# Layer norms turned by VectorE and DMA instead of TensorE, in a macaron transformer layer on one Trainium2 core

## The chip, the cores and the metric

The kernel runs on one core of a Trainium2 chip (trn2). The metric is device time in microseconds (us) of one execution, taken as the median of several runs. A core has five engines that run side by side, each in the order of its own instruction list: TensorE (PE; its weight loads are listed apart as PEld), VectorE (DVE), ScalarE (ACT), GpSimd (POOL) and the queue engine SyncE (SP), which here only issues DMAs. SPq and ACTq stand for the DMAs issued from SP and from ACT.

## The reference

One layer in fp32 on x of 8 sequences, 512 tokens and 128 features: half a feed-forward, an attention with 16 heads, and half of the same feed-forward again.

```python
x = x + 0.5 * ffn(layernorm(x))
x = x + attn(layernorm(x), Q, K, VO)
x = x + 0.5 * ffn(layernorm(x))

def ffn(x):                     # three residual blocks, six 128x128 linears
    h = x
    for blk in range(3):
        y = qlora_linear(h, 2 * blk)            # int4 weights with scales + low-rank part + bias
        y = gelu(layernorm(y) * gamma[blk] + beta[blk])
        h = qlora_linear(y, 2 * blk + 1) + h
    return h
def attn(x, Q, K, VO):          # rank 64 per head
    scores = (x Q^T) (x K^T)^T / sqrt(128);  out = sum over heads of softmax(scores) x VO
```

The six weight matrices are dequantized and joined with their low-rank parts once, at the start (`wT`).

## The kernel before

All 8 sequences stay in SBUF (`xs`), token-major: partition p holds 4 tokens. The attention sets the frame. Two heads make a pair, 8 pairs a sequence, 64 pairs in all; two pairs make a **turn**, and 32 turns (numbered s = 0 to 31, four to a sequence) follow each other. A turn has eight chunks, c0 to c3 of its first and its second pair; below they are called chunks 0 to 7 of the turn. For each chunk PE computes scores `ps` (L752) into one of two PSUM buffers, tag "scores"; DVE takes the negated row maxima `nm` (L759); ACT computes `e` = exp with the row sums `den` (L764); DVE inverts them (`rden`, L771); POOL divides one half of `e` (L776) and ACT the other (L778); DVE transposes `e` in blocks of 32x32 into `tr` (L792); and 16 DMAs per pair on SP (L848) put the blocks where they belong, as `eT`. One turn later PE multiplies them with the values into `acc` (L869).

The two feed-forwards and the attention's own layer norm run in the gaps of these turns. A feed-forward of one sequence is a `Unit`: it has an input norm, three `Block`s, and a final add. In a block PE multiplies `hT` by the first weights (`py`, L387), DVE adds the bias row (`y`, L394) and takes mean and variance (L352, L354), POOL computes `rstd` by a power of -0.5 (L360), DVE subtracts the mean and scales (`z`, four instructions of 128x128, L365), PE transposes `z` in four 128x128 transposes into PSUM (`p`, L334), ACT applies gamma, beta and Gelu (`aT`, L412), PE multiplies by the second weights (`po`, L419), and DVE adds bias and residual (`hT`, L425). The input norm of a Unit goes the same way with `z_n`, `p_n`, and a copy by ACT (L431); the attention's input norm with `z_an`, `p_an` and the copy `axT` (L620). Gelu and exp need different tables on ACT: each Gelu group is followed by `exp_again`, which loads exp's table back (L187).

The order on each engine is written out by hand. `at(t, fn)` files a task under a due time t; a turn is `SUP` = 32 such units; `run_tasks` emits all tasks sorted by t, and a dependency of each instruction on the one before it on its engine keeps that order. So a due time is a place in each engine's list, not a clock: an instruction that waits holds up everything behind it on its engine. `TIMES` has the due times of the eight chunks, `T_FIRST` those of the first half of a block, and `lay_start` those of a Unit's input norm.

Which norms fall into which turn repeats every four turns. In the middle of the kernel the turns with s mod 4 = 0, 1 and 2 each turn two norms, and those with s mod 4 = 3 three: one block's, the attention's (`z_an`), and the input norm of the front feed-forward (`z_n`, due at t + 16.58, sequences 3 to 7). In turns 0 and 2 (mod 4) both are blocks' norms, scaled at the turn's start (due 35.5 to 36.2 of the turn before) and transposed together after the last scores; turn 1 has a block's and the input norm of the back feed-forward (`z_n`, due t + 4.7).

Of the kernel before, what the change touches and what calls it, by code (L numbers as in the profile page):

```python
# [18 lines left out]
def kernel(  # L19
# [45 lines left out]
    small = ctx.enter_context(tc.tile_pool(name="small", bufs=8))  # L65

# [52 lines left out]
    la = [const.tile([LR, G, D], F32, name=f"la{i}") for i in range(2)]  # L119
# [93 lines left out]
    w = [const.tile([P, G, NG, GROUP], F32, name=f"w{i}") for i in range(2)]  # L213
# [3 lines left out]
    nat = const.tile([P, 2, P], F32, name="nat")  # L217

# [120 lines left out]
    class Norm:  # L339


        def __init__(self, src, name, tag):
            self.src, self.name, self.tag = src, name, tag
# [18 lines left out]
        def scale(self):  # L362
            z = work.tile([P, NC, D], F32, tag="z", name=f"z_{self.name}")
            for c in range(self.n):
                nc.vector.tensor_scalar(  # L365
                    z[:, c, :], self.src[:, c, :], self.mv[:, c, 0:1],
                    self.rstd[:, c : c + 1],
                    ALU.subtract, ALU.mult,
                )
# [4 lines left out]


    hTs = {}

    class Block:


        def __init__(self, f, k, b, tag):
            self.k, self.b, self.tag, self.name = k, b, tag, f"{f}_{k}_{b}"

        def first(self):
            self.py = bank(f"py{self.name}", self.tag)
            for c in range(NC):
                nc.tensor.matmul(  # L387
                    self.py[:, c, :], lhsT=hTs[self.b][:, c, :], rhs=wT[:, 2 * self.k, :],
# [3 lines left out]
        def biased(self):  # L392
# [4 lines left out]
            self.norm = Norm(y, self.name, self.tag)  # L397
# [10 lines left out]

        def gelu(self):
# [3 lines left out]
                self.aT, self.norm.p, AF.Gelu,  # L413
# [15 lines left out]
    def ffn_start(n, f, b):  # L429
        hTs[b] = work.tile([P, NC, P], F32, tag="hT", name=f"hT{f}_{b}", bufs=3)  # L430
        nc.scalar.copy(hTs[b], n.p)  # L431
# [138 lines left out]
    class Unit:  # L570


        def __init__(self, f, b):
            self.f, self.b, self.tag = f, b, f"g{f}"
            self.n = Norm(xs[b], f"n{f}_{b}", self.tag)

        def lay_start(self, times, tag=None):
# [3 lines left out]
            for at_n, (fn, *args) in zip(times, (  # L581
                (self.n.stats,), (self.n.root,), (self.n.scale,), (self.n.turn,),
# [4 lines left out]
        def lay_blocks(self, s, i, other={}):  # L587
# [6 lines left out]
            for k in range(NB):  # L594
                m = Block(self.f, k, self.b, self.tag)
# [5 lines left out]
                for x, fn in zip(other.get(("second", k)) or (  # L601
                    17.65 + 0.1 * i, 22.0 + 0.1 * i, 26.0, 25.4 + 0.8 * i, 26.3 + 0.8 * i
                ), (m.turn, m.gelu, exp_again, m.second, m.add)):
                    if x:
                        at(s * SUP + x, fn)
# [8 lines left out]
    def lay_attn_input(b, t):  # L614

        n = Norm(xs[b], f"an{b}", "g0")

        def keep():
            xTs[b] = work.tile([P, NC, P], F32, tag="xT", name=f"axT{b}", bufs=2)
            nc.scalar.copy(xTs[b], n.p)  # L620
# [3 lines left out]
        at(t + 4.7, n.scale)  # L624
        at(t + 17.65, n.turn)
# [25 lines left out]
    T_EARLY, T_LATE = (28.9, 29.7, 32.3, 35.6), (31.4, 32.0, 33.8, 36.0)  # L651
    T_FIRST = (
        (T_EARLY, None), (T_EARLY, (24.2, 25.0, 26.8, 35.5)), (None, T_EARLY),
        ((25.5, 26.5, 28.5, 35.5), T_EARLY), (T_EARLY, T_LATE),
# [229 lines left out]
    def attn_add(b, a):  # L884
        oT = work.tile([P, NC, P], F32, tag="oT", name=f"oT{b}", bufs=2)
# [400 lines left out]
```

## Time and profile before

| what | value |
|---|---|
| time, median of 3 runs | 1071.25 us (1071.16 to 1071.37) |
| profiled execution, first to last instruction | 1068.9 us |
| what lies around the span, taken as median less span | 2.35 us |
| PE busy | 1053.8 us (99%), granted clock 1.000 |
| DVE busy | 873.2 us (82%) |
| ACT busy | 793.9 us (74%) |
| POOL busy | 485.1 us (45%) |
| SP's DMA queue q1 | 139.94 MB, 57.0% of 16 engines |

The profiled execution has no time of its own beside its span; the difference of 2.35 us to the median of the runs is what is assumed to lie around it. Busy time is the union of an engine's instructions. A group's line gives source line, engine, operation, output from input, shapes and count, then busy time and mean length of one; instructions of a group overlap, so four transposes take less than four times their mean length. A line of a timeline gives start, length, engine, line, operation, count, and in brackets the idle time just before it with what ended it. A line of the waits gives who waited for whom: total us, times, longest.

### The profile page before, as it was taken

How to read it: one execution, taken by the hardware profiler on the slowest of the kernel's cores; microseconds unless marked ns; L12 is line 12 of the kernel's file. 1: busy time of each engine (PE TensorE's matmuls, PEld its weight loads, DVE VectorE, ACT ScalarE, POOL GpSimd, SP SyncE). 2: the span in 40 equal slices, each digit the busy share in tenths (PEclk: the TensorE clock that was granted, in tenths of full speed). 3: DMA queues.
4: the chain of work that ended last, by engine and by line, in shares of the span. 5: the costliest groups of instructions: out<-in, count | busy, mean ns of one | idle time of the engine just before them, and what ended most of it. 6: DMA issues, size and time to landing. Idle time of an engine off the chain costs nothing.

```text
span 1068.9 us, 15650 instructions
## 1 busy us (share of the span) xinstructions
PE 1053.8 (99%) x4628; PEld 560.2 (52%) x4628; DVE 873.2 (82%) x1767; ACT 793.9 (74%) x1710; POOL 485.1 (45%) x368
## 2 busy tenths in 40 slices
PE   9899999999999999999999999999999999999998
PEld 7445554545555554555545555554555554455546
DVE  6897868788888888888889888888888888777765
ACT  4877787777777787777787777787777787777742
POOL 4554434545443454444445444455444445444423
PEclk9999999999999999999999999999999999999999
DMA  6166655665576555566455566555567555566660
GB/s 189 38 141 138 158 129 132 140 141 128 120 167 158 121 117 119 129 158 158 110 130 126 122 155 155 131 124 122 117 152 167 126 125 117 131 145 158 158 158 21
DMA packets 58572, 142.40 MB, mean 133 GB/s; under 512 B 18732, under 2 KB 22904, under 8 KB 58488
## 3 DMA queue, kind: packets, MB, share of 16 engines
q1 hardware_dynamic: 56120, 139.94, 57.0%
q10 hardware_dynamic: 2368, 1.45, 0.6%
q8 instruction: 39, 0.64, 0.3%
q14 instruction: 45, 0.37, 0.1%
HBM read 5.01 MB, written 2.10 MB: 7 GB/s over the span
## 4 chain that ended last, share of the span: by engine, by line
PE 91%; DVE 3%; ACT 2%; SPq 2%; issue 1%; DMA 0%; POOL 0%; DVEq 0%; ACTq 0%; POOLq 0%
PE acc L869 37%; PE ps L752 20%; PE pqk L689 10%; PE pv L712 10%; PE po L419 4%; PE py L387 4%; PE p L334 2%; ACT e L764 2%; PE py L489 1%; SPq L848 1%; DVE tr L792 1%; DVE nm L759 1%; SPq L824 1%; PE sum L835 1%; PE p_n L334 1%; PE ph L334 1%
## 5 line engine op out<-in xcount | busy, mean ns | idle before, releaser
L776 POOL TENSOR_SCALAR e<-e,rden 128x512 f32<-128x512 f32 x257 | 399.5, 1564 | 336.1 <-DVE rden L771 336.1
L764 ACT ACTIVATE e<-ps,nm 128x512 f32<-128x512 f32 x512 | 345.0, 685 | 157.5 <-DVE nm L759 151.5
L869 PE MATMUL acc<-eT,v 64*128 64x512 f32 (+1 forms) x1756 | 457.8, 590 | 0.7 <-DMA eT<-tr 0.7
L759 DVE TENSOR_REDUCE nm<-ps 128x2 f32<-128x1024 f32 x256 | 299.6, 1206 | 47.9 <-PE ps L752 47.7
L792 DVE STREAM_TRANSPOSE tr<-e 128x1024 f32<-128x1024 f32 x252 | 307.8, 1231 | 29.9 <-POOL e L776 21.9
L869 PEld LDWEIGHTS acc<-eT,v 64*128 64x128 f32 (+1 forms) x1756 | 192.2, 187 | 216.9 <-issue 215.1
L752 PE MATMUL ps<-qk 64*128 64x512 f32 x1024 | 248.1, 598 | 2.8 <-ACT e L764 1.8
L778 ACT ACTIVATE e<-e,rden 128x512 f32<-128x512 f32 x255 | 176.0, 726 | 15.2 <-DVE rden L771 13.9
L752 PEld LDWEIGHTS ps<-qk 64*128 64x128 f32 x1024 | 94.6, 186 | 126.2 <-issue 83.3
L712 PE MATMUL pv<-vo_sb,axT 128*128 128x256 f32 x512 | 121.7, 380 | 0.3 <-ACT e L764 0.3
L712 PEld LDWEIGHTS pv<-vo_sb,axT 128*128 128x128 f32 x512 | 94.8, 190 | 28.7 <-issue 12.4
L360 POOL TENSOR_TENSOR rstd<-mv,mhalf 128x4 f32<-128x4 f32 x42 | 42.9, 1022 | 146.7 <-DVE mv L354 145.9
L764 ACT ACTIVATION_READ_ACCUMULATOR e<-ps,nm 128x1 f32 x512 | 103.6, 202 | 0.0
L725 ACT COPY v<-pv 128x512 f32<-128x512 f32 x124 | 66.8, 594 | 42.0 <-PE pv L712 42.0
L771 DVE RECIPROCAL rden<-den 128x2 f32<-128x2 f32 x256 | 41.4, 165 | 36.3 <-ACT e L764 35.4
L695 ACT COPY qk<-pqk 128x1024 f32<-128x1024 f32 x61 | 61.0, 1000 | 3.9 <-PE pqk L689 3.9
L689 PE MATMUL pqk<-axT,qT_w 128*128 128x512 f32 x122 | 63.3, 601 | 0.2 <-ACT e L764 0.2
L689 PE MATMUL pqk<-axT,kT_w 128*128 128x512 f32 x122 | 62.3, 592 | 0.0
L387 PEld LDWEIGHTS py<-wT,hT 128*128 128x128 f32 x336 | 42.3, 191 | 13.0 <-DVE hT L425 9.2
L365 DVE TENSOR_SCALAR z<-y,mv,rstd 128x128 f32<-128x128 f32 x168 | 48.1, 356 | 0.6 <-POOL rstd L360 0.6
L394 DVE TENSOR_TENSOR y<-py,bias_bc 128x512 f32<-128x512 f32 x42 | 28.7, 683 | 22.6 <-PE py L387 22.0
L387 PE MATMUL py<-wT,hT 128*128 128x128 f32 x336 | 45.4, 278 | 1.0 <-DVE hT L425 0.8
(143 smaller groups left out, 724.0 us busy)
## 6 DMA issues: line engine op xcount, KB each, us to landing
eT<-tr SPq DMA_DIRECT2D x1008, 128.0 KB, 2.3
x<-in_L_attn_x_dram SPq DMA_DIRECT2D x7, 256.0 KB, 6.0
out_dram<-x SPq DMA_DIRECT2D x7, 256.0 KB, 2.4
eT<-tr SPq DMA_DIRECT2D x16, 64.0 KB, 2.0
eT<-tr ACTq DMA_DIRECT2D x16, 64.0 KB, 2.1
qk_sb<-in_L_attn_Q_dram SPq DMA_DIRECT2D x1, 448.0 KB, 4.4
qk_sb<-in_L_attn_K_dram SPq DMA_DIRECT2D x1, 448.0 KB
x<-in_L_attn_x_dram SPq DMA_DIRECT2D x2, 128.0 KB, 2.8
```

The lines of the kernel that those rows point to most:

```text
L387: nc.tensor.matmul(self.py[:, c, :], lhsT=hTs[self.b][:, c, :], rhs=wT[:, 2 * self.k, :], start=True, stop=True,)
L689: nc.tensor.matmul(self.pg[:, i, :], lhsT=(qT_w, kT_w)[i][:, self.g, :], rhs=xTs[self.b], start=True, stop=True,)
L695: nc.scalar.copy(self.qk, self.pg)
L712: nc.tensor.matmul(p, lhsT=xTs[self.b][:, c, :], rhs=vo_sb[:, 2 * self.g : 2 * self.g + 2, :], start=True, stop=True,)
L725: nc.scalar.copy(self.v[:, c : c + NC // 2], self.pv[:, c : c + NC // 2])
L752: nc.tensor.matmul(ps[:, j, :], lhsT=self.qk[rows, 0, ts(c, P)], rhs=self.qk[rows, 1, :], start=True, stop=True,)
L759: nc.vector.tensor_reduce(self.nm[:, c, :], self.ps[c], AX.X, ALU.max, negate=True)
L764: nc.scalar.activation(e[:, j, :], self.ps[c][:, j, :], AF.Exp, bias=self.nm[:, c, j : j + 1], accum_out=self.den[:, c, j : j + 1],)
L776: nc.gpsimd.tensor_scalar(e, e, r, None, ALU.mult)
L778: nc.scalar.activation(e, e, AF.Copy, scale=r)
L792: nc.vector.transpose(self.tr[:, :, :, c, :], self.e[c].rearrange("p h (k j r) -> p j (h k) r", j=Q4, r=32),)
L869: nc.tensor.matmul(accs[self.b][i], lhsT=self.v[rows, k, j, :], rhs=self.eT[rows, :, j * NC + k, :], start=first, stop=end and (j == 1 or ...
```

## The change

Three things are changed. First, the norms that are transposed for a turn s > -1 (all but the input norms of sequences 1 and 2 of the front feed-forward, the first block of sequence 1, and the last block of sequence 6 of the back one) are no longer transposed by PE. VectorE transposes `z` in 32x32 blocks into a buffer `zout` (`spread`, one instruction of 128x512). Once per turn an `Exchange` writes the buffer of all its norms (two or three of 256 KB) to DRAM with one DMA, and reads it back with four DMAs, one for each 32 partitions, such that the blocks land transposed (`zin`). All five are issued from SP, due at 8.0 of the turn. ACT's Gelu and copies read `zin` in SBUF instead of `p` in PSUM.

Second, `z` of these norms is computed on GpSimd instead of VectorE. Input norms still subtract and scale; blocks' norms only multiply by `rstd`, since the first weights and biases are centred once at the start (`sums`, `centered`): each output column's mean over the features is taken away, so that `y` has mean zero. Due times move: the scaling follows the root at once, `spread` is due 3.6 to 3.7 into the turn (5.45 for the back feed-forward's block in turns 3 mod 4, 7.5 for its input norm). The front feed-forward's input norm has its statistics moved one turn ahead (due 26.9 of turn s-2, where it was 27.0 of turn s-1), its root and scaling to 16.0 of turn s-1.

Third, room is made: the start's weight tiles `la` and `w` share a buffer with the exchange (tag "zx"), and `oT` has one buffer instead of two.

```diff
+        dram = tc.tile_pool(name="dram", bufs=2, space=bass.MemoryType.DRAM)
+    def sums():
+        first = wT.rearrange("p (k two) o -> p k two o", two=2)[:, :, 0, :]
+        for i, src in enumerate((first, bias_bc)):
+            nc.vector.tensor_reduce(less[:, i, :], src, AX.X, ALU.add)
+    def centered():
+        nc.gpsimd.tensor_scalar(less, less, -1.0 / D, None, ALU.mult)
+        for i in range(2):
+            for k in range(NB):
+                nc.gpsimd.tensor_scalar(
+                    bias_bc[:, k, :] if i else wC[:, k, :],
+                    bias_bc[:, k, :] if i else wT[:, 2 * k, :],
+                    less[:, i, k : k + 1], None, ALU.add,
+                )
...
         def scale(self):
+            engine = nc.gpsimd if self.exchange else nc.vector
             for c in range(self.n):
-                nc.vector.tensor_scalar(
+                if self.centered:
+                    engine.tensor_scalar(
+                        z[:, c, :], self.src[:, c, :], self.rstd[:, c : c + 1], None, ALU.mult
+                    )
+                    continue
+                engine.tensor_scalar(
                     z[:, c, :], self.src[:, c, :], self.mv[:, c, 0:1],
                     self.rstd[:, c : c + 1],
                     ALU.subtract, ALU.mult,
...
+        def spread(self):
+            nc.vector.transpose(
+                self.exchange.out()[:, :, self.slot, :, :],
+                self.z.rearrange("p c (j r) -> p j c r", r=32),
+            )
+        def turned(self):
+            if self.exchange:
+                return self.exchange.landed[:, :, self.slot, :, :].rearrange("p i c q -> p c i q")
+            return self.p.rearrange("p c (i q) -> p c i q", q=32)
+    class Exchange:
...
+        def run(self):
+            f = self.n * NC * 32
+            far = dram.tile([P, Q4, f], F32, tag="far", name=f"far{self.s}")
+            nc.sync.dma_start(out=far, in_=self.sent.rearrange("p j a c q -> p j (a c q)"))
+            self.landed = self.tile("zin")
+            for j in range(Q4):
+                nc.sync.dma_start(
+                    out=self.landed[32 * j : 32 * (j + 1)].rearrange("p i a c q -> p i (a c q)"),
+                    in_=far.rearrange("(i r) j f -> j r i f", r=32)[j],
+                )
+    SPREAD = (3.6, 3.7)
...
-                    self.py[:, c, :], lhsT=hTs[self.b][:, c, :], rhs=wT[:, 2 * self.k, :],
+                    self.py[:, c, :], lhsT=hTs[self.b][:, c, :], rhs=wC[:, self.k, :],
...
-                self.aT, self.norm.p, AF.Gelu,
+                self.aT.rearrange("p c (i q) -> p c i q", q=32), self.norm.turned(), AF.Gelu,
...
+                    if far and fn == m.turn:
+                        at(s * SUP + (5.45 if i and s % 4 == 3 else SPREAD[i]), m.spread)
...
-        at(t + 4.7, n.scale)
-        at(t + 17.65, n.turn)
+        at(t + 0.3, n.scale)
+        at(t + 3.65, n.spread)
...
-    T_EARLY, T_LATE = (28.9, 29.7, 32.3, 35.6), (31.4, 32.0, 33.8, 36.0)
+    T_EARLY, T_LATE = (28.9, 29.7, 32.3, 32.4), (31.4, 32.0, 33.8, 33.9)
...
+    at(-0.55, sums)
+    at(-0.5, centered)
...
-            m.lay_start((t - 5.0, t + 1.1, t + 16.58, t + 20.3, t + 20.7))
+            m.lay_start((t - 2 * SUP + 26.9, t - SUP + 16.0, t - SUP + 16.1, t + 3.6, t + 20.7))
...
-            m.lay_start((t + 0.1, t + 1.1, t + 4.7, t + 17.65, t + 17.85))
+            m.lay_start((t + 0.1, t + 1.1, t + 1.2, t + 7.5, t + 17.85))
```

## The prediction

> **What bounds the kernel now.** I read the page first, then the groups, then the list of waits, and then the timeline of whole turns, engine by engine.
>
> The page's busy line (us, share of the span, instructions) names TensorE, and the largest group of transposes that the change removes (busy us, mean ns, idle us before) sits on it:
>
> ```profile
> PE 1053.8 (99%) x4628; PEld 560.2 (52%) x4628; DVE 873.2 (82%) x1767; ACT 793.9 (74%) x1710; POOL 485.1 (45%) x368
> ```
> ```profile
> L334 PE MATMUL p<-ident,z 128*128 128x128 f32 x168 | 24.4, 279 | 1.3 <-DVE z L365 1.3
> ```
>
> Read alone, this says that every us taken from PE is a us gained. The list of waits (total us, times, longest) says something else:
>
> ```profile
> ACT aT L412 <- PE p L334: 13.3, 1, 13.3
> ...
> PEld pqk L689 <- ACT qk L695: 11.8, 27, 0.6
> ...
> PEld po L419 <- ACT aT L412: 6.8, 22, 1.0
> ```
>
> Gelu waited for PE's transposes once in 42 times (at the start), but PE's weight loads waited for Gelu's result 22 times and for ACT's copy of q and k 27 times. The order in time shows why. Turn 8 (s mod 4 = 0, from 275.9 us), PE and its weight loads, then ACT:
>
> ```profile
> 293.36 1.09 PE L334 MATMUL p<-ident,z 128*128 128x128 f32 x8
> 294.29 3.60 PE L869 MATMUL acc<-eT,v 128*128 128x512 f32 x8
> ...
> 301.16 1.92 PE L419 MATMUL po<-aT,wT 128*128 128x512 f32 x4
> ```
> ```profile
> 301.10 0.30 PEld L419 LDWEIGHTS po<-aT,wT 128*128 128x128 f32 x2 [0.18 <-ACT aT L412]
> ...
> 302.67 0.44 PEld L689 LDWEIGHTS pqk<-axT,qT_w 128*128 128x128 f32 x2 [0.42 <-ACT qk L695]
> ```
> ```profile
> 294.78 0.69 ACT L764 ACTIVATE e<-ps,nm 128x512 f32<-128x512 f32 x1 [0.85 <-DVE nm L759]
> ...
> 298.98 1.28 ACT L412 ACT_TABLE_LOAD   x1
> ...
> 300.27 1.45 ACT L412 ACTIVATE aT<-p,gb 128x512 f32<-128x512 f32 x2
> ...
> 301.61 1.01 ACT L695 COPY qk<-pqk 128x1024 f32<-128x1024 f32 x1
> ```
>
> From 294.78 to 302.6 ACT has no gap: exps of chunks 6 and 7, two divisions, table, two Gelus, copy of q and k. PE needs the Gelus for `po` and the copy for its next scores buffer. So the second half of a turn is set by when DVE releases chunk 6 (the 0.85 us wait for `nm`), and PE, which had the transposes to do meanwhile, arrives at `po` within 0.1 us of ACT. Two chains of equal length run there, and only one gets shorter.
>
> Where does chunk 6's `nm` wait? In turns 8, 9 and 10 it follows DVE's own `tr` without a gap; in turn 11 (s mod 4 = 3) something of the change stands before it. DVE and ACT of turn 11:
>
> ```profile
> 388.05 1.23 DVE L792 STREAM_TRANSPOSE tr<-e 128x1024 f32<-128x1024 f32 x1
> 389.20 1.19 DVE L365 TENSOR_SCALAR z_n<-x,mv_n,rstd_n 128x128 f32<-128x128 f32 x4
> 390.32 2.34 DVE L759 TENSOR_REDUCE nm<-ps 128x2 f32<-128x1024 f32 x2
> ```
> ```profile
> 391.62 0.69 ACT L764 ACTIVATE e<-ps,nm 128x512 f32<-128x512 f32 x1 [1.23 <-DVE nm L759]
> ```
>
> **The change, part by part.** Everything is summed against the profiled span, 1068.9 us; the median of the runs is 2.35 us more.
>
> *PE's transposes removed.* 59 norms (40 of blocks, 7 of the attention, 5 and 7 input norms) times four are 236 transposes. Eight hold PE from 293.36 to 294.29, 0.116 us each, so 27.4 us of PE. On the path I count what PE's arrival was late: `pqk` started at 302.93 where the copy ended at 302.62 and its weights could load at 302.67, so about 0.07 us a turn, 30 turns: -2.0 us. Ends: 0 and -27.4. I take the low one because the two weight loads above already wait for ACT.
>
> *`z_n` leaves DVE before chunk 6.* The four scalings take 389.20 to 390.32, 1.12 us, straight on the chain `tr`, `nm`, exp, table, Gelu, `po`. The scores of chunk 6 are there sooner: PE began them at 387.30, the first half takes 0.86. PE follows, as without its twelve transposes it ends `acc` at about 391.6. This happens in the turns of sequences 3 to 7: 5 x 1.12 = -5.6 us. End: 0, if ACT's `axT` copy, which stands before exp 6, has to wait for its data instead.
>
> *Other scalings leave DVE, `spread` comes.* One `tr` of 128x1024 is 1.23 us, so a `spread` of 128x512 is about 0.62 (0.75 with a fixed part). In turn 10 eight scalings took 2.13 us after the first two `nm`; two spreads take 1.25. But the next `nm` waited 0.6 us for PE's scores there, so nothing comes of it: 0. In turn 9 the later `spread` of the back input norm comes between `nm` of chunk 3 and its `rden`, where DVE waits 0.44 us for exp: 0.62 less 0.44 eats the 0.2 us that chunk 2's `nm` gains. 0.
>
> *GpSimd's scaling, and who waits for it.* In turn 11 POOL's list now reads root (attention), four scalings with two operations, root (block), four with one, and only then the first division:
>
> ```profile
> 371.22 1.03 POOL L360 TENSOR_TENSOR rstd_an<-mv_an,mhalf 128x4 f32<-128x4 f32 x1 [7.05 <-DVE mv_an L354]
> 372.99 1.01 POOL L360 TENSOR_TENSOR rstd<-mv,mhalf 128x4 f32<-128x4 f32 x1 [0.74 <-DVE mv L354]
> ...
> 377.06 1.58 POOL L776 TENSOR_SCALAR e<-e,rden 128x512 f32<-128x512 f32 x1 [2.09 <-DVE rden L771]
> ```
>
> A division of 512 columns takes 1.56 us. A quarter of it is 0.39; with a fixed part of about 0.12 (two memsets, 24 columns 0.141 us and 216 columns 0.278) it is 0.48. That is my value for one operation; for two I take 0.60, between 0.48 and twice that. 371.22 + 1.03 + 2.40 + 1.01 + 1.94 = 377.6, and the block's `spread` ends at 378.2; DVE's `nm` of chunk 2 stands behind it and began at 378.35. So 0, with ends: scalings at 0.39 let it start when PE's scores are there (378.05), 7 x -0.3 = -2; at 0.53 and 0.97 the `spread` ends at 379.9, 7 x 1.5 = +10.8. In other turns POOL has at most one norm before a `spread`, and the first `tr` comes 3 us after its division, so a division 0.5 us late is hidden. The root and scaling of the front input norm, moved to 16.0 of turn 10, fall between 358.25 and 361.07, where POOL is idle 2.81 us; they need 3.4, so division 6 is 0.6 late, `tr` of chunk 7 too, and behind it `hT`, which waited 0.78 for PE: hidden. Its statistics (1.25 us) go into a gap of DVE of 1.25 us in turn 9.
>
> The Trainium skill, page "GPSIMD Engine Reference", section "Engine selection", speaks against this step: elementwise work belongs on VectorE, with GpSimd about twice as slow for two inputs and near line rate for one. Its section "Performance versus the Vector engine" measures 769 ns for 512 elements in the best case, and by that a scaling would be an estimated 0.19 us and the term -2; the division's 1.56 us in this trace is twice the page's figure, and the trace decides.
>
> *The exchange.* 59 x 256 KB go out and come back, some 30 MB beside q1's 140. SP gets five issues a turn at about 0.6 us each, and its four reads wait for the write to land. In turn 9, the tightest, the last `spread` ends at about 317.5; SP is idle from 314.5 to 325.8. A 256 KB store lands in 2.4 us, so 512 KB in about 3.6; four reads of 128 KB are issued in 2.4 and the last lands 2.3 (as `eT`) to 3.3 later: 325.2 to 326.5. SP is free again at 323.5, before the next `eT` DMA. ACT's copy of `hT`, due before exp 6, must start by 326.3. I take 0.1 us of wait in seven such turns: +0.7; ends 0 and +7 (reads 1 us later). In turn 11 768 KB land at about 388.8, needed at 389.7. In turns 8 and 10 the Gelus come at 300 and 364, with 7 us to spare.
>
> *ACT reads SBUF.* A division by ACT (SBUF, 726 ns) against an exp (PSUM, 685 ns), both with a column operand, gives 0.04 us more; 40 Gelus on ACT's chain: +1.6. Ends: 0, and 0.11 (0.61 between two divisions against 0.50 between two copies of v), +4.4.
>
> *Start.* `sums`, two reductions of 128x384, stand directly before the first `nm` (29.73, right behind `z_n`). At `nm`'s 1.2 us per 1024 columns that is 0.5 us each: +1.0 (ends +0.5, +1.5). `centered` lies in POOL's idle time up to 32.8 and delays a first division by 1 to 2 us, which its `tr` at 41.19 doesn't notice.
>
> Sum: -2.0 - 5.6 + 0 + 0 + 0.7 + 1.6 + 1.0 = -4.3: a span of 1064.6, a time of 1067.
>
> **The rivals.**
>
> *PE is the bound, as its 99% says.* Then all 27.4 us less the start's 1.0 are gained: 1045. For it: PE has 15 us of gaps in the whole span. Against: the waits of its weight loads, which the busy share hides.
>
> *GpSimd holds DVE (slower).* In the three-norm turns DVE waits at the block's `spread` with `nm`, and with it exp, queued behind. Each us that POOL's eight scalings take beyond 4.3 delays seven turns, and beyond 5.1 us (0.48 for one operation, 0.8 for two) it eats the 5.6 us. At 6.0 us: -4.3 + 10.8 = +6.5, 1078. For it: the division is slow on POOL. Against: 0.48 leaves 0.15 us to spare.
>
> *The round trip is late.* If the reads land 1.5 us later than reckoned, turns with a copy before exp 6 lose some 1.3 us: 7 x 1.3 in turns 1 mod 4, and the 5.6 of turns 3 mod 4 shrink to 2: -4.3 + 8.4 + 3.6 = +7.7, 1079. Against: DRAM traffic is only 7 GB/s, and SP is idle when it is issued.
>
> *Nothing is left.* Gelu from SBUF at its upper end, and 0.5 us lost in turn 9, cancel the gain: 1071.
>
> **How the numbers follow.** Chances: forecast 0.42, PE bound 0.08, GpSimd 0.22, round trip 0.15, nothing 0.13. This measurement tells 0.2%, about 2.1 us, from no change. Faster: the forecast and the PE case, 0.50. Same 0.14: the case of nothing left, and a little from the slower ones. Slower 0.36. The likeliest case alone reaches from 1059 to 1071. The range runs to 1049, leaving only the full PE case below, and to 1083, where GpSimd's upper end (+10.8) meets some of the others' costs.
>
> **What would show it.** Right: PE's busy share falls by some 2.5 points while `po` and `pqk` wait longer for ACT, about 0.9 us a turn; in turns 3 mod 4 exp 6 starts about 1.1 us earlier after the turn's first scores. Wrong: PE still without waits and the span down by 20; DVE's `spread` waiting for POOL's `z`; ACT's `axT` or `hT` waiting for a DMA; the start waiting on weights, whose tiles now share a buffer.

## The result, and the profile after

| | before | after |
|---|---|---|
| time, median (lowest to highest) | 1071.37 us (1071.13 to 1073.08, 9 runs) | 1073.01 us (1072.66 to 1076.57, 9 runs) |
| ratio to before | | 1.0025, 95% interval 1.0014 to 1.0035 |
| profiled execution, first to last instruction | 1068.9 us | 1071.0 us |

The changed kernel is a little slower: +1.6 us by the medians, +2.1 us between the two profiled executions, where -4.3 had been forecast. The measured direction is that of the rival "GpSimd holds DVE". The page's line on the engines, after (us, share of the span, instructions):

```profile
PE 1041.5 (97%) x4392; PEld 534.2 (50%) x4392; DVE 843.9 (79%) x1592; ACT 792.3 (74%) x1710; POOL 642.2 (60%) x611
```

PE is busy 12.3 us less and DVE 29.3 us less; POOL is busy 157 us more. In the chain of work that ended last, before and then after (shares of the span by engine):

```profile
PE 91%; DVE 3%; ACT 2%; SPq 2%; issue 1%; DMA 0%; POOL 0%; DVEq 0%; ACTq 0%; POOLq 0%
```
```profile
PE 49%; DVE 16%; ACT 12%; SPq 10%; POOL 5%; DMA 4%; issue 4%; DVEq 0%; ACTq 0%; POOLq 0%
```

PE alone carried the end before; now PE shares it with DVE, ACT and POOL. The changed kernel's list of waits says who waits for whom (total us, times, longest). PE's weight loads wait for Gelu 21.0 us in 40 places, where it was 6.8 in 22, and VectorE's `spread` (`zout`) waits for GpSimd's scalings:

```profile
PEld po L508 <- ACT aT L501: 21.0, 40, 1.5
PEld pqk L784 <- ACT qk L790: 14.0, 27, 0.6
```
```profile
DVE zout L408 <- POOL z L393: 12.4, 9, 1.5
DVE zout L408 <- POOL z_an L397: 4.0, 5, 1.3
```

**Where the time went, turn by turn.** From the start of each turn's first scores on PE to that of the next, summed by s mod 4 (turns 0 and 1 apart), profiled executions:

| us | before | after | difference |
|---|---|---|---|
| up to the first scores | 28.39 | 28.90 | +0.51 |
| turns 0 and 1 | 63.54 | 64.64 | +1.10 |
| seven turns s mod 4 = 0, from 4 | 219.63 | 218.48 | -1.15 |
| seven turns 1, from 5 | 217.06 | 215.11 | -1.95 |
| eight turns 2 | 251.37 | 250.02 | -1.35 |
| seven turns 3 | 223.58 | 228.11 | +4.53 |
| from the last turn's first scores to the end | 65.33 | 65.74 | +0.41 |

The turns 0, 1 and 2 mod 4 that transpose two norms each got 0.2 to 0.3 us shorter. Of the turns 3 mod 4, numbers 11, 15, 19 and 23 take 32.91 us instead of 32.27, and number 27, which has no `z_n`, 32.38 instead of 30.58. (Number 3 takes 32.08 instead of 31.64, and number 7, which has `z_n`, 32.03 instead of 32.27.)

**A turn with two norms** (turn 8, PE, its weight loads and ACT in the changed kernel; start, length, operation, in brackets the idle time before it and what ended it):

```profile
302.07 1.98 PE L508 MATMUL po<-aT,wT 128*128 128x512 f32 x4 [0.34 <-ACT aT L501]
```
```profile
302.07 0.30 PEld L508 LDWEIGHTS po<-aT,wT 128*128 128x128 f32 x2 [0.74 <-ACT aT L501]
302.78 0.45 PEld L508 LDWEIGHTS po<-aT,wT 128*128 128x128 f32 x2 [0.41 <-ACT aT L501]
```
```profile
295.72 0.69 ACT L859 ACTIVATE e<-ps,nm 128x512 f32<-128x512 f32 x1 [0.85 <-DVE nm L854]
...
301.20 1.52 ACT L501 ACTIVATE aT<-zin,gb 128x512 f32<-128x512 f32 x2
302.63 0.99 ACT L790 COPY qk<-pqk 128x1024 f32<-128x1024 f32 x1
```

PE, rid of its eight transposes, now waits for Gelu before `po`; ACT runs from exp 6 on without a gap, as before. The 0.85 us wait for `nm` is the same to the digit.

**A turn with three norms** (turn 11, POOL and DVE in the changed kernel):

```profile
371.62 1.03 POOL L386 TENSOR_TENSOR rstd_an<-mv_an,mhalf 128x4 f32<-128x4 f32 x1 [5.65 <-DVE mv_an L380]
373.39 1.01 POOL L386 TENSOR_TENSOR rstd<-mv,mhalf 128x4 f32<-128x4 f32 x1 [0.73 <-DVE mv L380]
374.40 3.13 POOL L397 TENSOR_SCALAR z_an<-x,mv_an,rstd_an 128x128 f32<-128x128 f32 x4
377.51 2.36 POOL L393 TENSOR_SCALAR z<-y,rstd 128x128 f32<-128x128 f32 x4
```
```profile
377.57 0.71 DVE L408 STREAM_TRANSPOSE zout<-z_an 128x512 f32<-128x512 f32 x1 [0.67 <-POOL z_an L397]
...
379.90 0.71 DVE L408 STREAM_TRANSPOSE zout<-z 128x512 f32<-128x512 f32 x1 [1.51 <-POOL z L393]
380.54 2.31 DVE L854 TENSOR_REDUCE nm<-ps 128x2 f32<-128x1024 f32 x2
```

The maxima of chunk 2 before the change:

```profile
378.35 2.33 DVE L759 TENSOR_REDUCE nm<-ps 128x2 f32<-128x1024 f32 x2
```

From 372.65 to 373.39 POOL waits for the block's `mv`, and the attention norm's scaling, whose data are there, is queued behind that wait. The two scalings then take 3.13 and 2.36 us. VectorE waits 0.67 and 1.51 us at its two `spread`s, and `nm` of chunk 2 begins 8.39 us after the turn's first scores (372.15); before it was 6.60 (378.35 less 371.75). That is 1.79 us later.

### The profile page after: what moved, and what is told of

Its sections match the earlier page's. It is cut to its first block, busy times and chain, and to the rows that moved or that the text cites. A ratio compares the mean times of both kernels' runs of the same rounds, so it can differ in the third digit from the quotient of the medians.

```text
span 1071.0 us, 15598 instructions
## 1 busy us (share of the span) xinstructions
PE 1041.5 (97%) x4392; PEld 534.2 (50%) x4392; DVE 843.9 (79%) x1592; ACT 792.3 (74%) x1710; POOL 642.2 (60%) x611
## 3 DMA queue, kind: packets, MB, share of 16 engines
q10 hardware_dynamic: 2368, 1.45, 0.6%
## 4 chain that ended last, share of the span: by engine, by line
PE 49%; DVE 16%; ACT 12%; SPq 10%; POOL 5%; DMA 4%; issue 4%; DVEq 0%; ACTq 0%; POOLq 0%
PE acc L964 17%; PE ps L847 11%; SPq L943 9%; DVE tr L887 7%; ACT e L859 7%; PE pqk L784 6%; DVE nm L854 5%; PE pv L807 5%; PE po L508 4%; DMA eT<-tr 3%; ACT L501 2%; POOL z L393 2%; PE py L473 2%; POOL z_an L397 2%; ACT aT L501 1%
## 5 line engine op out<-in xcount | busy, mean ns | idle before, releaser
L847 PE MATMUL ps<-qk 64*128 64x512 f32 x1024 | 252.2, 602 | 8.8 <-ACT e L859 7.0
L807 PEld LDWEIGHTS pv<-vo_sb,axT 128*128 128x128 f32 x512 | 94.7, 190 | 29.3 <-issue 8.9
L393 POOL TENSOR_SCALAR z<-y,rstd 128x128 f32<-128x128 f32 x160 | 94.3, 609 | 3.3
L866 DVE RECIPROCAL rden<-den 128x2 f32<-128x2 f32 x256 | 36.4, 144 | 50.4 <-ACT e L859 49.4
L508 PE MATMUL po<-aT,wT 128*128 128x512 f32 x84 | 43.9, 627 | 7.3 <-ACT aT L501 7.2
L473 PEld LDWEIGHTS py<-wC,hT 128*128 128x128 f32 x336 | 42.3, 191 | 12.3 <-DVE hT L514 7.1
L473 PE MATMUL py<-wC,hT 128*128 128x128 f32 x336 | 45.1, 277 | 0.9 <-DVE hT L514 0.9
```

The source lines that it names most:

```text
L393: engine.tensor_scalar(z[:, c, :], self.src[:, c, :], self.rstd[:, c : c + 1], None, ALU.mult)
L473: nc.tensor.matmul(self.py[:, c, :], lhsT=hTs[self.b][:, c, :], rhs=wC[:, self.k, :], start=True, stop=True,)
L807: nc.tensor.matmul(p, lhsT=xTs[self.b][:, c, :], rhs=vo_sb[:, 2 * self.g : 2 * self.g + 2, :], start=True, stop=True,)
L847: nc.tensor.matmul(ps[:, j, :], lhsT=self.qk[rows, 0, ts(c, P)], rhs=self.qk[rows, 1, :], start=True, stop=True,)
```

## The experiments

Each kernel is a change of one of the two kernels. Runs of before on the same chips had medians of 1071.17 to 1071.50 us; the ratios are against them.

### e1: the block's spread behind the scores of the second pair

```diff
-  at(s * SUP + (5.45 if i and s % 4 == 3 else SPREAD[i]), m.spread)
+  at(s * SUP + (7.5 if i and s % 4 == 3 else SPREAD[i]), m.spread)
```

> The changed kernel with one due time moved: in the turns 3 mod 4 the block's spread is due 7.5 instead of 5.45, so it stands behind the maxima of chunks 2 and 3 instead of ahead of them. Theory H (GpSimd holds DVE: the spread waits 1.5 us for POOL's z, with nm and exp queued behind): chunk 2's nm starts 2.1 us sooner, the spread itself costs 0.2 us later, and the exchange is sent some 2 us later, which may make ACT's axT copy wait 0.5 us: 1.4 us in each of seven turns, 1060 to 1064 us instead of 1073. Rival T (the round trip through DRAM is late): sending it later makes it worse, up to 7 x 1.2, 1073 to 1081. Rival P (PE is the bound): 1073.

Measured: 1062.13 us (1060.98 to 1064.06), ratio 0.9916 (0.9901 to 0.9930). The seven turns 3 mod 4 take 216.77 us instead of 228.11: -11.3 us, 1.6 us in each on average (0.9 in turn 7, 1.5 to 1.9 in the others); every other group of turns stays within 0.15 us but turn 0, of which more below. VectorE in turn 11 (first scores at 371.12):

```profile
377.45 2.36 DVE L854 TENSOR_REDUCE nm<-ps 128x2 f32<-128x1024 f32 x2
379.72 0.70 DVE L408 STREAM_TRANSPOSE zout<-z 128x512 f32<-128x512 f32 x1
```

`nm` comes 6.33 us after the first scores, ahead of the `spread`, and the `spread` follows it without a wait, with POOL's list and GpSimd's durations unchanged. One due time thus turns the change from 0.25% slower to 0.8% faster. The hold is shown, and its size: 11.3 us is what the place of this `spread` ahead of `nm` cost. What is late next shows in the waits of ACT in e1 (none of this kind in the changed kernel):

```profile
ACT axT L715 <- DMA zin<-far: 5.0, 5, 1.1
```

The later `spread` sends the exchange off later, and in the five turns with `z_n` the copy `axT` now waits about 1 us for the round trip. PE in turn 11 of e1 has no wait in its second half, so this one is hidden there.

### e6: only the order on POOL

```diff
-        at(t + 0.3, n.scale)
+        at(t + 0.25, n.scale)
```

> The changed kernel with one due time altered: the attention norm's scaling at t + 0.25 instead of t + 0.3, so that on POOL it stands ahead of the block's root, which waits for VectorE's mv. Theory (the order on POOL's list is part of the hold): z_an starts at the end of its own root (372.7 instead of 374.4 in turn 11), the block's root follows at about 375.8, its four scalings end at about 379.1 instead of 379.9, so the block's spread and nm of chunk 2 come 0.7 to 1.1 us earlier in seven turns: -5 to -7.5 us, a time of 1065.5 to 1068. Rival (the order doesn't matter, since POOL's work up to the block's spread is as much in either order, and only the scalings' size counts): the turns 3 mod 4 stay at 32.9 us, 1073.

Measured: 1070.51 us (1068.44 to 1072.56), ratio 0.9992 (0.9982 to 1.0002). POOL in turn 11 (first scores at 371.32):

```profile
371.93 3.13 POOL L397 TENSOR_SCALAR z_an<-x,mv_an,rstd_an 128x128 f32<-128x128 f32 x4
375.03 1.03 POOL L386 TENSOR_TENSOR rstd<-mv,mhalf 128x4 f32<-128x4 f32 x1
376.16 2.36 POOL L393 TENSOR_SCALAR z<-y,rstd 128x128 f32<-128x128 f32 x4
```

`z_an` starts 1.64 us earlier in the turn's own time (0.61 us after the first scores instead of 2.25), but the block's root now stands behind it and starts at 375.03 instead of at 373.39. POOL ends the block's scaling at 378.5, and `nm` begins 7.86 us after the first scores instead of 8.39. The turns 11, 15, 19, 23 and 27 get 0.52 us shorter, turn 7 1.0, the group 3.6 us in all. (The median moves by 2.5 us only, since more of its executions fell under the drop of the clock told of below.) So the order is about a third of the hold; the lower end of what was expected was 0.7 us a turn. The rest of the hold is put down to the scalings' length; no run has shorter scalings on GpSimd.

### e2: the transposes put back on PE, unread

```diff
     if far and fn == m.turn:
         at(s * SUP + (5.45 if i and s % 4 == 3 else SPREAD[i]), m.spread)
+        at(s * SUP + x, m.turn)
...
+    if self.n.exchange:
+        at(times[4] - (0.2 if self.f else 0.4), self.n.turn)
...
     at(t + 3.65, n.spread)
+    at(t + 17.65, n.turn)
```

> The changed kernel with the 236 TensorE transposes put back at their old due times, writing to PSUM banks that nobody reads; everything else as changed. Two equal chains (PE had these transposes while ACT was on its way to Gelu, so taking them away was worth 0.07 us a turn): 0 to +3 us, 1073 to 1076. Rival P (PE is the bound, and the 27 us were gained and lost again elsewhere): +27, 1100.

Measured: 1082.94 us (1082.62 to 1085.27), ratio 1.0115 (1.0099 to 1.0132): +9.9 us on the changed kernel, +9.8 between the profiled spans (1080.8 against 1071.0). The turns 0, 1 and 2 mod 4 with two norms get 0.2 to 0.3 us longer, the five with three 0.89; numbers 3 and 27, which have two, do not change. This lies between the two theories: the transposes hold PE for 27 us, a good third of it was on the path, and my 0.07 us a turn was far too little.

### e7: both, the late spread and the transposes on PE

> The kernel of e1_late_spread, in which VectorE no longer waits for GpSimd, with the 236 transposes on PE put back beside the exchange, their result unread. It shows what they are worth once the hold is gone. Theory (the chain through DVE and ACT and PE's own work are nearly equal in every turn, so each part of the change is worth something only where the other has shortened its chain too): +0.25 us in turns 0, 1 and 2 mod 4 as in e2, and +1.0 or more in turns 3 mod 4, where the chain is now 1.8 us shorter and twelve transposes are 1.4 us of PE: +13 to +16 us on 1062, that is 1075 to 1078. Rival (what the transposes cost does not depend on the hold): +9.9 us, 1072. Rival (PE alone is the bound): +27, 1089.

Measured: 1071.48 us (1070.28 to 1076.79), ratio 1.0007 (0.9994 to 1.0020). By groups of turns, against e1 and against before:

| us | before | e1 | e7 |
|---|---|---|---|
| turns 0 mod 4 | 219.63 | 218.44 | 219.60 |
| turns 1 mod 4 | 217.06 | 215.26 | 217.02 |
| turns 2 mod 4 | 251.37 | 249.97 | 251.31 |
| turns 3 mod 4 | 223.58 | 216.77 | 222.50 |

With the transposes back, three of four groups are as before within 0.06 us: the exchange, the scalings on GpSimd and the `spread`s, without PE's relief, are worth nothing there and cost nothing. The transposes are worth 10.0 us over the four groups without the hold (e7 less e1) and 9.1 with it (e2 less the changed kernel). The 0.9 us between them are mainly the net of two things. Turn 5, which varies between 29.2 and 29.9 us among the profiled executions, counts 0.7 less without the hold than with it. The turns 3 mod 4 count 1.35 more, and most of that is one turn: number 15 of e7 takes 33.03 us where 7, 11, 19 and 23 take 32.10 to 32.11. ACT's timeline has there

```profile
523.22 0.62 ACT L718 COPY axT<-zin 128x512 f32<-128x512 f32 x1 [2.82 <-DMA zin<-far]
```

which is the round trip again, this time not hidden. The `spread` is no later there than in e7's other turns; the write took longer: the four reads, which wait for it, were issued 5.07 us after it (517.51 and 512.44), against 3.30 us in turn 11 of e1. Why it took longer is open. In the four other turns with three norms the transposes cost 0.88 to 1.01 us, about as in e2. So the theory was wrong and the rival right: what PE's transposes cost hardly depends on the hold. The waits of `po` for `aT` and of `pqk` for `qk`, 21.0 and 14.0 us in the changed kernel, in e7:

```profile
PEld po L508 <- ACT aT L501: 6.1, 19, 1.1
PEld pqk L788 <- ACT qk L794: 8.3, 23, 0.6
```

They are back at or below the 6.8 and 11.8 us of the kernel before: with the transposes PE is the later one in most turns.

### e3: z_n off VectorE, the transposes kept

The kernel before, with the front norm's statistics, root and scaling moved one turn ahead and the scaling on GpSimd.

```diff
+  engine = nc.gpsimd if self.ahead else nc.vector
...
-  m.lay_start((t - 5.0, t + 1.1, t + 16.58, t + 20.3, t + 20.7))
+  m.n.ahead = True
+  m.lay_start((t - 2 * SUP + 26.9, t - SUP + 20.9, t - SUP + 20.95, t + 20.3, t + 20.7))
```

> The kernel before with one part of the change alone: the front feed-forward's input norm (sequences 3 to 7) has its statistics, root and scaling one turn earlier, the scaling on GpSimd where POOL is idle after the last division (due 20.95), so that no z_n stands before the maxima of chunk 6 on DVE. TensorE still transposes. The prediction's step: 5 x 1.12 us, 1071.4 - 5.6 = 1065.8. Rival P: PE's work is the same, 1071.4.

Measured: 1071.33 us (1070.64 to 1073.12), ratio 0.9999 (0.9990 to 1.0008). VectorE does what was expected of it: in turn 11 (first scores at 373.92) the second half's `nm` follows `tr` directly, and exp 6 starts 1.1 us earlier in the turn. The turn gets 0.16 us shorter (32.10 instead of 32.26). PE in turn 11 of e3, and then of before:

```profile
394.80 0.60 PE L334 MATMUL p_n<-ident,z_n 128*128 128x128 f32 x4
...
398.68 1.06 PE L390 MATMUL py<-wT,hT 128*128 128x128 f32 x8
399.57 1.02 PE L422 MATMUL po<-aT,wT 128*128 128x512 f32 x2
400.43 1.02 PE L692 MATMUL pqk<-axT,qT_w 128*128 128x512 f32 x2
```
```profile
392.62 0.60 PE L334 MATMUL p_n<-ident,z_n 128*128 128x128 f32 x4
...
396.67 1.05 PE L387 MATMUL py<-wT,hT 128*128 128x128 f32 x8
397.63 1.12 PE L419 MATMUL po<-aT,wT 128*128 128x512 f32 x2
398.60 1.07 PE L689 MATMUL pqk<-axT,qT_w 128*128 128x512 f32 x2
```

In neither does PE wait (no brackets): with twelve transposes to do, PE arrives at `po` when the Gelus are there anyway. Exp 6 waiting 1.23 us for `nm` was true, but PE did not wait behind it. The seven turns 3 mod 4 together get 0.8 us shorter, the four groups only 0.2.

### e4: the round trip left out

```diff
-            at(s * SUP + 8.0, x.run)
+            at(s * SUP + 8.0, x.stay)
...
+        def stay(self):
+            self.landed = self.sent
```

> The changed kernel without the exchange: no DMA out and none back, ACT reads the spread blocks as they lie in zout. This leaves out the crossing of blocks between partitions, so what is computed is not the reference. Theory H: no instruction of ACT waited for the trip in the profile, so only SP's issues and some 30 MB of DMA traffic go: 0 to -2 us, 1071 to 1073. Rival T: the trip holds ACT's copies in the turns 1 and 3 mod 4, -7 us or more, 1066 or less.

Measured: 1074.99 us (1073.36 to 1076.91), ratio 1.0033 (1.0020 to 1.0046). All groups of turns are within 0.2 us of the changed kernel's: as it was changed, the trip through DRAM costs nothing in them. The kernel is not faster but 2 us slower by the median; in the profiled execution this lies in the last 30 us: PE waits longer for the last `eT` there (2.59 us instead of 1.72) and then runs slowly, which no theory had foreseen. Its one execution without such a slow stretch took 1073.4 us, 0.4 to 0.7 us above those of the changed kernel. The last two groups of experiments are about that.

### e5 and e8: what is left on POOL, and the start

e5 is e1 with the order of e6 and the front norm's root and scaling moved behind the last division of their turn (from due 16.0 and 16.1 to 20.9 and 20.95).

> The kernel of e1_late_spread (block's spread in turns 3 mod 4 due 7.5 instead of 5.45), with POOL's list reordered in two places: the attention norm's scaling ahead of the block's root (t + 0.25 instead of t + 0.3), and the front input norm's root and scaling due 20.9 and 20.95 of the turn before instead of 16.0 and 16.1, behind the last division. Theory: the hold is gone already by the later spread, so nothing is left to gain there; the division of chunk 6 in turns 2 mod 4 is no longer 2 us late, but this was hidden; 1060 to 1063, equal to e1 within 1 us. Rival (GpSimd's divisions still delay DVE's tr): another 0.3 us in five to seven turns, 1058 to 1060.

Measured: 1064.71 us (1062.80 to 1065.47), ratio 0.9931 (0.9917 to 0.9944). The four groups of turns take 900.8 us, those of e1 900.4: nothing is left to gain on POOL, as expected. The time is 2.6 us above e1's nevertheless, and its reason lies elsewhere: in the profiled execution 2.3 us before the first scores (30.96 us instead of 28.65). All five of its executions also show a drop of the clock, of e1's four only two; see below for both.

e8 is e5 with the centring moved; `sums` and `centered` are split there into the weights' part (0) and the biases' (1):

```diff
-    at(-0.55, sums)
-    at(-0.5, centered)
+    at(1.2, sums, 0)
+    at(1.25, centered, 0)
+    at(3.85, sums, 1)
+    at(5.45, centered, 1)
```

> e5_combined with the centring at the start moved: the sums of the weights between the first two nm (due 1.2), those of the biases at 3.85, GpSimd's additions behind them (1.25 and 5.45), so that the first nm follows z_n directly, as before the change. Theory: the 0.83 us that turn 0 lost come back mostly, 0.5 to 1 us on e5_combined. Rival (py, which needs the centred weights, then waits for GpSimd, as it began at 38.13 and the additions end at about 36): nothing gained or up to 1 us lost.

Measured: 1062.13 us (1060.93 to 1063.04), ratio 0.9913 (0.9899 to 0.9926). Turn 0 takes 30.49 us; it was 31.19 in the changed kernel and 30.36 before, so 0.7 of the 0.8 us come back. `py` did not wait for the centred weights. The median moves by 2.6 us, more than was expected of the start: only two of e8's four executions show a drop of the clock.

### e9 and e10: the clock

In e1, e5 and e7 turn 0 took 32.6 us instead of the changed kernel's 31.2, with the same instructions. PE in turn 0 of the changed kernel, and then of e5:

```profile
33.91 1.13 PE L847 MATMUL ps<-qk 64*128 64x512 f32 x4 [1.44 <-ACT e L859]
35.25 1.13 PE L847 MATMUL ps<-qk 64*128 64x512 f32 x4 [0.21 <-ACT e L859]
36.31 1.12 PE L767 MATMUL pq<-axT,qT_w 128*128 128x512 f32 x2
```
```profile
35.97 1.13 PE L847 MATMUL ps<-qk 64*128 64x512 f32 x4 [1.43 <-ACT e L859]
37.31 1.71 PE L847 MATMUL ps<-qk 64*128 64x512 f32 x4 [0.21 <-ACT e L859]
38.95 2.07 PE L767 MATMUL pq<-axT,qT_w 128*128 128x512 f32 x2
```

The same matmuls after the same wait take up to 1.8 times as long. The windows of e5 (window, length, busy time of PE, PEld, DVE, ACT, POOL, then the granted clock, DMA share and GB/s) show why, and those of e6 show the same at the end of the kernel:

```profile
33.00:37.00 4.00, 2.57 (x12) 0.84 (x12) 2.73 (x4) 2.97 (x9) 3.50 (x7) 1.00 0.00 0
37.00:42.00 5.00, 4.79 (x12) 1.82 (x11) 3.81 (x8) 3.50 (x10) 4.69 (x5) 0.66 0.00 0
```
```profile
1036.00:1040.00 4.00, 1.79 (x6) 0.73 (x5) 2.94 (x14) 0.00 (x0) 1.03 (x1) 1.00 0.71 173
1040.00:1044.00 4.00, 4.00 (x14) 3.29 (x13) 0.00 (x0) 0.00 (x0) 0.00 (x0) 0.57 0.14 33
```

Us by us the clock stands at 0.50 for some 3.4 us and then at 1.00 again. Two waits of PE come before it: one of 1.44 us in turn 0, because the first `nm` stands behind the two `sums` (before the change it was 0.51), and one of 1.6 to 2.6 us for the last `eT` at the end (1.56 before the change). In the profiled executions the drop came after a wait of 1.44 us in turn 0 (e1, e5, e7) and after waits of 2.2 to 2.6 us at the end (e4, e6, e7). To test whether PE's idleness is the cause, e9 fills the second wait, and e10 both, with matmuls that nobody reads; e9 starts from e8, e10 from e5, whose late start stays.

```diff
+    for i in range(10):                                   # e9, e10
+        at(t + 19.9, lambda: nc.tensor.transpose(end_sums[1][:, :P], ident, ident))
...
+    for i in range(10):                                   # e10
+        at(1.96, lambda: nc.tensor.transpose(first.p[:, 3, :], first.z[:, 3, :], ident))
```

> The kernel of e8_start (late spread, POOL's order, centring moved) with ten transposes of the unit matrix on PE, their result unread, ahead of the ten sum matmuls at the end, where PE waits 1.7 to 2.6 us for the last eT DMAs. Theory (a wait of PE of 1.4 us or more is what lets the granted clock fall to 0.50 some us later, in part of the executions): the wait shrinks to about 0.6 us, and no execution shows a mean clock under 0.9995: its times lie at 1060.5 to 1061.5 without the ones at 1063. Rival (the clock falls for another reason, or at any wait there): the times still spread over 2 us, 1062.

> The kernel of e5_combined (centring still ahead of the first nm) with ten such transposes at the end as in e9_filled and ten more in turn 0, behind p_n, where PE waits 1.44 us for exp. Nothing at the start is sooner: the first nm still stands behind the two sums. Theory (it is PE's idleness that drops the clock, not the late start itself): turn 0 takes 31.2 us in every execution, never 32.6, the mean clock is 1.000, and the time is that of e9 plus the 0.7 us by which turn 0 is longer: 1061 to 1062.5. Rival: turn 0 still takes 32.6 us in part of the executions, 1063 to 1065 as e5.

Measured: e9 1061.62 us (1060.74 to 1064.16), ratio 0.9911 (0.9896 to 0.9926); e10 1062.01 us (1061.36 to 1064.62), ratio 0.9914 (0.9899 to 0.9928). PE at the end of e9:

```profile
1029.37 1.26 PE L1260 MATMUL sum<-ident 128*128 128x128 f32 x10
1031.02 2.40 PE L928 MATMUL sum<-eT,v 128*128 128x256 f32 x10 [0.39 <-issue]
```

The mean granted clock of each execution tells the rest:

| kernel | executions with a mean clock under 0.999 | times at 0.999 or more | times under 0.999 |
|---|---|---|---|
| before, beside e1 to e10 | 0 of 44 | 1070.6 to 1073.4 | |
| after | 4 of 9 | 1072.7 to 1073.0 | 1075.0 to 1076.6 |
| e1 | 2 of 4 | 1061.0 to 1062.0 | 1062.3 to 1064.1 |
| e2 | 2 of 4 | 1082.6 to 1082.7 | 1083.2 to 1085.3 |
| e3 | 0 of 10 | 1070.6 to 1073.1 | |
| e4 | 4 of 5 | 1073.4 | 1073.9 to 1076.9 |
| e5 | 5 of 5 | | 1062.8 to 1065.5 |
| e6 | 7 of 11 | 1068.4 to 1069.4 | 1070.4 to 1072.6 |
| e7 | 4 of 11 | 1070.3 to 1071.7 | 1073.3 to 1076.8 |
| e8 | 2 of 4 | 1060.9 to 1061.3 | 1062.9 to 1063.0 |
| e9 | 0 of 5 | 1060.7 to 1064.2 | |
| e10 | 0 of 5 | 1061.4 to 1064.6 | |

With the waits filled no mean clock was under 0.999 (one in e9 was 0.999, the others 1.000; the drop of 3.4 us alone makes 0.998), and e10's turn 0 took 31.20 us although its first `nm` is as late as e5's: it is PE's waiting that lets the clock fall. What decides between two executions with the same wait can be read off the profiled ones, though no run tests it. In their records of the granted clock every stretch between two changes is a whole multiple of 3.413 us (1064.96 us is 312 of them, 27.31 is 8), so the clock changes on a grid of that period, and the grid lies differently against the kernel in each execution. At the end e5, e6 and e7 wait 2.21 us each. In e6 and e7 2.1 us or more of it fell into one period of the grid, and the clock dropped at that period's end; in e5 the grid cut the wait in two, 1.48 us the larger part, and it did not drop. In turn 0 it dropped where one period held 1.64 us or more without a matmul (e1, e5, e7), not where it held 1.62 or less (the changed kernel, e2, e4, e6); that margin is thin, and at the end 1.96 us (e2) were not enough, so no single number follows.

The times of e9 and e10 still spread by more than 3 us, as e9's rival had it, though not for its reason: some are 2 us and more above the rest at full clock, as are some of the kernel before (1073 among 1071). In the profiled executions of e3, e5 and e7 the first scores began some 2 us later than elsewhere (30.55 to 30.96 us instead of 28.4 to 29.2). The same matmul early in the kernel before, and then in e3:

```profile
5.98 0.27 PE L478 MATMUL pp<-ident,pz 128*128 128x128 f32 x1
```
```profile
7.00 0.42 PE L481 MATMUL pp<-ident,pz 128*128 128x128 f32 x1
```

The records of the granted clock begin, at 1.00, when the matmuls get short: at 10.0 to 10.5 us in e3, e5 and e7, at 3.9 to 6.4 us in the nine others. So PE starts slow in every profiled execution and in these three stays so for 3.5 us or more longer; the mean granted clock, which counts from the first record on, does not show it (e3: 1.00). That this is also what e9's and e10's longer times are was not seen in a profile.

e8 and e9 are the best versions found, 0.9% under the kernel before and 1.0% under the changed one; e1, with one due time changed, and e10 are equal to them within the intervals.

## Why the prediction was wrong, point by point

**GpSimd's scalings (forecast 0, measured +11.3 us: the step that failed).** This term alone decides the direction: without the hold the change is 0.8% faster (e1). Two errors add up. The lengths: I took 0.48 us for a scaling with one operation and 0.60 for one with two. The group of the changed kernel's POOL (busy us, mean ns of one; overlapping instructions, so four take 2.36 and 3.13 us):

```profile
L871 POOL TENSOR_SCALAR e<-e,rden 128x512 f32<-128x512 f32 x257 | 399.4, 1567 | 218.7 <-DVE rden L866 218.5
L393 POOL TENSOR_SCALAR z<-y,rstd 128x128 f32<-128x128 f32 x160 | 94.3, 609 | 3.3
L397 POOL TENSOR_SCALAR z_an<-x,mv_an,rstd_an 128x128 f32<-128x128 f32 x28 | 21.9, 797 | 0.1
```

They are 0.59 and 0.78 us. For a quarter of the division's columns that is a fixed part of about 0.27 us ((4 x 0.59 - 1.56) / 3), twice what I had drawn from two memsets, and a second operation costs 0.19. Eight scalings took 5.49 us instead of 4.34, 1.15 more. The order: I listed root, scaling, root, scaling, but by the due times (the block's root is due 32.3 of the turn before, the attention norm's scaling 0.3 of this one, filed later) both roots come first, and the second waits for VectorE. e6 gives 0.52 us for it. Together 1.67 us; less the 0.15 us of slack that is 1.52 of the 1.79 us by which `nm` moved. The rival had the mechanism, the place and the price (+10.8 at its upper end); its lengths were given as the range's end (0.53 and 0.97), and its sum was +6.5, 4 to 5 us too much, because it took over the forecast's too small gain from PE's transposes. That its price came out is in part luck: its lengths add up to 6.0 us for the eight scalings, and the measured 5.49 us comes to that only with the wait that the order added. Both were within reach: "0.15 us to spare" on a path of 6.4 us is no cover. The Trainium skill, page "GPSIMD Engine Reference", section "Engine selection", says that elementwise work belongs on VectorE, and the trace agrees: the four scalings of `z_n` took 1.12 us there, and 3.13 on GpSimd. The best case of its section "Performance versus the Vector engine", an estimated 0.19 us for a scaling, was missed by a factor of three.

**PE's transposes (forecast -2.0, measured -9 to -10 us).** That PE would then wait for Gelu was right: 0.74 and 0.41 us at the weight loads of `po` in turn 8, and not all 27 us were gained. The mechanism was right too; the term was mis-sized: I read how late PE was in one turn (0.07 us, turn 8) and took it for all. Gelu and `po` of turn 12, before (first scores at 404.02) and after (405.06):

```profile
428.00 1.45 ACT L412 ACTIVATE aT<-p,gb 128x512 f32<-128x512 f32 x2
429.19 1.88 PE L419 MATMUL po<-aT,wT 128*128 128x512 f32 x4
```
```profile
429.04 1.52 ACT L501 ACTIVATE aT<-zin,gb 128x512 f32<-128x512 f32 x2
429.91 1.98 PE L508 MATMUL po<-aT,wT 128*128 128x512 f32 x4 [0.34 <-ACT aT L501]
```

Gelu starts 23.98 us after the first scores in both, `po` 25.18 and then 24.85 us after them, and `pqk` behind it 26.89 and then 26.67. So PE came 0.33 us late to `po` and 0.22 late to `pqk`, and the turn got 0.23 us shorter. In e7's turn 19, with twelve transposes, `po` comes 0.76 us later in the turn than in e1's, while Gelu starts within 0.03 us of it; that turn is 0.90 us longer.

**z_n off VectorE (forecast -5.6, measured -0.8 alone).** The 0.8 us are those of the turns 3 mod 4; the time did not change. The wait of exp 6 was real and went away (in e3's turn 11 exp 6 follows the copy `axT` without a wait, where it waited 1.23 us), but PE, busy without a gap from 388 to 404 us, set the end of that turn. I had followed the chain to `po` in turn 8 and assumed it in turn 11. Only with both parts, and without the hold, do the turns with three norms lose 1.0 to 1.3 us (e1). The two terms together were forecast at -7.6; the four groups of turns of e7's table add up to 911.6 us before and 900.4 in e1, -11.2. So the gain was there, and larger than forecast, but for another reason: nearly all of it comes from PE's transposes. Over the whole span the -11.2 us and the hold's +11.3 cancel, and +1.6 at the start and +0.4 at the end make the +2.1 us.

**The exchange (forecast +0.7, measured 0).** e4 shows that the turns do not depend on it. ACT never waited for `zin`; 512 KB landed 2.8 us after their issue, and the four reads 2.8 after theirs. The rival's mechanism is real, though: where the write is issued 0.8 us later in the turn and the copy is due sooner, as in e1 and e7, `axT` waits for the reads.

**The `spread`s, Gelu from SBUF, other edits at nothing.** A `spread` took 0.70 us, between the 0.62 and 0.75 named. A Gelu group from SBUF takes 1.52 us for two instead of 1.45, 0.04 each as worked out. In turn 10 the delayed division 6 stayed hidden, as argued. e7 shows that all of these together cost nothing in three groups of turns.

**The start (forecast +1.0, measured +1.6).** The sums took 0.55 us each, as the estimate of 0.5 had it, and turn 0 grew by 0.83; turn 1 grew by 0.27 in every variant of the changed kernel, and the first scores came 0.5 us later. These last 0.5 us are not shown to be the change's: the variants' first scores lie between 28.65 and 29.18 us where the clock rises early, and of the kernel before there is one profile. That PE's longer wait there can cost another 1.4 us through the clock was in no step.

**The time around the span.** I had put 2.35 us between span and time. It is 1.8 in every later execution (1072.78 and 1071.0): the profiled execution of before was a little under its median. That is 0.5 us of the forecast.

## What to carry to other kernels

Follow a wait to the engine that sets the end before counting it: exp 6 waited, yet nobody waited behind it, and an engine with a busy share of 99% and no waits in a stretch is the one to relieve there. When work moves to another engine, write that engine's list out by the due times, with the waits at the head of each item, and take its durations from an instruction of the same size: 0.15 us of slack on a sum of estimates is a coin toss. When such work holds a consumer, move the consumer's place in its own queue first; one due time was worth 11 us here.

## What the runs showed of the hardware that was not expected

- PE's granted clock fell to 0.50 for about 3.4 us after a wait of PE of 1.4 us or more, in part of the executions (after a wait of 1.4 us in turn 0 in three of the seven profiled executions that have it; after one of 2.21 us at the end in e6 and e7, not in e5). It cost 1.4 us at the start and 1.6 to 1.7 us at the end, and with the wait filled by unread matmuls none of ten executions showed it. The changes lie on a grid of 3.413 us, and in these profiles the drop followed where enough of the wait fell into one period. The Trainium skill, page "TensorE: Matmul & The Clock Gate", section "What's actually happening", tells of a gate at half clock with a free-running window of about 3.4 us: the length, the half clock and the grid agree with these traces; the wait that was enough is shorter than the idle window named there.
- At the start PE's clock reached 1.00 at 3.9 to 6.4 us in nine profiled executions and at 10.0 to 10.5 us in three; the first scores of these three came 1.4 to 2.6 us later.
- GpSimd has a high fixed cost in scalings of 128x128: 0.59 us with one operation and 0.78 with two, against 1.56 for 128x512 with one.
- The exchange of three norms (turn 11 of e1) took 9.0 us from its write's issue at 380.45 us to the copy that waited for its reads: by the medians of the changed kernel 768 KB landed in DRAM after 3.3 us, and the reads of 192 KB 3.8 us after their issue.
